# Two attention and feed-forward layers on one core: the first products of batch 14 over three heads, and the last layer's tokens in parts of 12 and 4 batches

## The chip, the cores and the metric

The kernel runs on one NeuronCore of one Trainium2 chip. The metric is the device time of one execution in microseconds (us); the time of the kernel before is 1855.08 us, the median of three runs (1853.94 to 1855.9). Batches and heads are counted from 0, so there are batches 0 to 15, and batch 14 is the next to last.

## The reference

The input `x` is 16 batches of 256 tokens with 256 features, and `ctx_1024` is a context of the same shape. Four layers follow one another, each added to `x`, each on the layer norm of `x`:

```python
x = x + xattn0(ctx_1024, layernorm(x), ...)   # 8 heads of 128, keys from the context and from x
x = x + ffn0(layernorm(x), ...)               # hidden 1024, weights W1 and W2 changed per batch by 16 of its tokens
x = x + xattn1(layernorm(x), ctx_1024, ...)   # one head of 256
x = x + experts(layernorm(x), ...)            # 8 experts with inner size 256
```

In the last layer each token has a weight for each of the 8 experts, which comes from its own router logits `z`:

```python
inh = sigmoid(x @ Wr / temperature)
in_zone = (inh >= GOLDEN_LOWER) & (inh <= 0.5)
w = exp(-abs(inh - GOLDEN_CENTER) / 0.1) * in_zone
# a token with no expert in the zone takes its best two instead
out = sum_e weights[e] * (silu(x @ Wg[e]) * (x @ Wu[e])) @ Wd[e]
```

A token is served by an expert where that weight is above zero. How many tokens an expert serves is decided by the data alone; it is not fixed at two or at any other number.

## The kernel before, in words

The whole program is written out as straight-line code by one Python function. Its order on each engine is the order in which the Python code issues instructions, because the schedule is manual. There is one `if` on the chip, at the very end.

**Heads.** The outer loop runs over `n`, the 16 x 8 heads of the first layer, with a pipeline in three stages: `s1` makes scores, `s2` writes their transposes to DRAM and `s2_fetch` reads them back, `s3` multiplies with the values. While batch b is in its heads, the later layers of batch b-1 run as a *chain* (`chain`, a generator) and the routing of a batch as a second generator (`route`). Both stand in a list `line`; `gap()` is called between the pieces of a head and takes units from the first job in `line` that is ready. What "ready" means is planned: every `yield w` in a generator tells that it can go on when the planned TensorE time `Clock.pe` has grown by `w`. The planned time grows by every matmul that is issued, in units that are not those of the chip. So a larger `yield` puts other instructions ahead of the next unit, and nothing else; the true waits are semaphores.

**The chain's feed-forward part.** Eight products `ph` (`W1e` with the tokens) come in four pairs, each followed by `yield 1.0`. Behind the last pair ScalarE takes a Gelu over all of `hT` (line 475). The second products `pf` need `hT` and `W2e`; `W2e` is made by GpSimd (by VectorE for batch 15) at line 437 and added up by VectorE at line 445. Ahead of `pf` stands `yield done[0] - Clock.pe`, which is the planned end of the Gelu.

**Routing.** `route` finds for each token which experts serve it, counts with a matmul by a triangle of ones how many came before it, and so gives every served (token, expert) a slot. GpSimd then writes the token's row (256 features, 8 weights, its number) with an indirect DMA into `slots_d` (line 719), once for each expert. Tokens that an expert does not serve go to slots counted from the end. `slots_d` has two parts, by batch, given by `PARTS`. Each part has for each expert as many slots as tokens, of which the first half, `CAPS`, is worked through in any case:

```python
PARTS = (10, 6)
NTOKS = [n * S for n in PARTS]
CAPS = [n // 2 for n in NTOKS]
```

For parts of 10 and 6 batches the capacities are 1280 and 768 tokens, that is 10 and 6 tiles of 128 rows for each expert, 128 tiles for all.

**The last layer.** `experts` is a generator over a list of *groups*. A group is 1 to 4 tiles of one expert and part. Its rows are loaded (line 1138, SyncE's queue), transposed in blocks by VectorE, written to DRAM (line 296) and read back (line 302) as `yTd`; then come the products `pg` and `pu`, tanh on ScalarE (line 1201), two operations on VectorE (lines 1211 and 1212) and, one group later, the products `pd`, one for each tile, whose weighted result `o` (line 1227) is added to the output in DRAM by an indirect DMA from GpSimd (line 1228). The chain before has written `x` to the output; every scatter adds to it. Scatters of one part and expert never meet in a row, nor do those of different parts; a scatter waits for the scatters of another expert of its own part. The rows of part 1 are loaded only once batch 15 has been routed (`ready` in `experts`).

The list before is: part 0 in groups of 4, 3 and 3 tiles for each expert, except the last group of expert 7; then part 1 in groups of 3 and 3 for experts 0 to 6; then the last group of part 0; then part 1 of expert 7 in 3, 2 and 1.

**The `if`.** After all this VectorE takes the slot counters, subtracts the limits, and takes the maximum over both parts and all experts (lines 1364 to 1366). Every engine loads that number (line 1367) and compares it (line 1368). Where any expert has more tokens in a part than the capacity, the block runs, and works through the other half of all slots, of every expert and both parts, with the same `experts` generator:

```python
some = nc.values_load(beyond[0:1, 0:1], min_val=0, max_val=1)
with tc.If(some > 0):
    drain(experts(groups(0, "+", (4, 3, 3)) + groups(1, "+", (3, 3))))
```

Of the kernel before, what the change touches and what calls it, by code (L numbers as in the profile page):

```python
# [29 lines left out]
def xattn_ffn_kernel(  # L30
# [11 lines left out]
    B, S, D = x.shape  # L42
# [4 lines left out]
    E = Wg.shape[0]  # L47
# [20 lines left out]
    def mm_tile(n, name):  # L68
        return psum.tile([P, n], F32, tag="mm", bufs=6, name=name, padded_shape=[P, 512])
# [9 lines left out]
    def mm(out, lhsT, rhs, **kw):  # L79
        nc.tensor.matmul(out, lhsT, rhs, **kw)  # L80
        Clock.pe += max(0.38, 1.667e-3 * math.prod(out.shape[1:]))
# [76 lines left out]
    )  # L158


    PARTS = (10, 6)
    NTOKS = [n * S for n in PARTS]
    CAPS = [n // 2 for n in NTOKS]

# [51 lines left out]
    def col(key, i):  # L216
        k, r = at[key]
        return cvecs[k][:, r + i : r + i + 1]
# [97 lines left out]
    def advance(gen):  # L316
        return gen is not None and next(gen, DONE) is not DONE

    def drain(gen):
        while advance(gen):  # L320
            pass
# [10 lines left out]
    def chain(b, A, behind):  # L332
# [60 lines left out]
        def rows_everywhere(half):  # L393
            evs.append(wk.tile([P, NI, D], F32, tag="ev", name=f"ev_{half}_{b}"))
            nc.sync.dma_start(
                evs[half].rearrange("p n d -> p (n d)"),
                ev_d[ts(half, NI)].rearrange("n d -> (n d)").partition_broadcast(P),
            )
            landed.append(Clock.pe + 8.0)
# [27 lines left out]
        def w1_rows(i):  # L427
            for d in range(DC):
                nc.vector.scalar_tensor_tensor(
                    W1e[:, d, i, :], evs[0][:, i, :], od[:, d, i : i + 1], W1T[:, d, ts(i, D)],  # L430
                    ALU.mult, ALU.add,
                )
# [21 lines left out]
        for k in range(HC):  # L454
            ph = mm_tile(S, f"ph_{b}_{k}")
            for d in range(DC):
                mm(
                    ph, W1e[:, d].rearrange("p i a -> p (i a)")[:, ts(k, P)], yT[:, d],
                    start=(d == 0), stop=(d == DC - 1),
                )  # L460
            nc.vector.tensor_scalar(hT[:, k, :], ph, col("b1", k), None, ALU.add)
            if k % 2 == 1:
                i = k // 2
                if i + 2 < NI:
                    w1_rows(i + 2)
                yield 1.0
                if i == 1:
                    rows_everywhere(1)
        A.fed.add(b)

        done = []
# [14 lines left out]
            w2_add(c)  # L486
        while not done:
            yield 0.2
        yield done[0] - Clock.pe
        W2r = W2e.rearrange("p c d o -> p (c d) o")  # L490
        mv = mv_tile("q")
        for c in range(TC):
# [136 lines left out]
    def route(b, A, mine):  # L629
        while not mine.done or (b >= 1 and not A.tails[b - 1].done):  # L630
            yield 0.4
        part = 0 if b < PARTS[0] else 1
        row = A.row[b]
# [105 lines left out]
    with ExitStack() as sh, ExitStack() as sa, ExitStack() as sf:  # L739
# [352 lines left out]
        def add_chain(b, behind):  # L1092
            job = Job(chain(b, A, behind))
            A.tails[b] = Job(route(b, A, job))
            line.extend([job, A.tails[b]])
            return job
# [20 lines left out]
        def load_expert(e):  # L1117
            k = len(D_.w)
            pool = D_.front if k == 0 else D_.wk if k == 1 else D_.more
            w = D_.w[e] = pool.tile([P, 3, DC, D], F32, bufs=1, name=f"wx_{e}")  # L1120
            nc.sync.dma_start(w[:, 0], Wg[e].rearrange("(c p) i -> p c i", p=P))
            nc.sync.dma_start(w[:, 1], Wu[e].rearrange("(c p) i -> p c i", p=P))
            nc.sync.dma_start(w[:, 2], Wd[e].rearrange("(c p) d -> p c d", p=P))
# [113 lines left out]
        def experts(groups, ready=None):  # L1237

            if groups[0].e not in D_.w:
                load_expert(groups[0].e)  # L1240
            for g in groups[:2]:
                g.load()
            yield 7.0
            while D_.wk is None:
                yield 0.4
            for d in range(DC):
                groups[0].turn_rows(d)
                yield 4.0
            late = None
            for n, g in enumerate(groups):  # L1250
                if n == 0:
                    groups[2].load()
                if n + 3 < len(groups):
                    while ready is not None and not ready(groups[n + 3]):
                        yield 0.4
                for i in range(IC):
                    g.gate(i)
                    yield
                    g.up(i)
                    yield  # L1260
                    if n == 0:
                        groups[1].turn_rows(i)
                    if n + 2 < len(groups):
                        if i == 0:
                            groups[n + 2].send_rows()
                        else:
                            groups[n + 2].fetch_rows()
                    if i == 0 and n + 3 < len(groups):
                        groups[n + 3].load()
                    if late is not None:  # L1270
                        late.down(2 * i)
                        late.down(2 * i + 1)
                        yield
                ahead = groups[min(n + 3, len(groups) - 1)].e
                if ahead not in D_.w and (len(D_.w) < 2 or D_.more is not None):
                    load_expert(ahead)
                if n + 2 < len(groups) and groups[n + 2].e not in D_.w:
                    while D_.more is None:
                        yield 0.4
                    load_expert(groups[n + 2].e)  # L1280
                late = g
            for t in range(late.tiles):
                late.down(t)

        def groups(part, more, sizes, experts_=range(E)):

            gs = []
            for e in experts_:
                t = CAPS[part] // P if more else 0
                for k in sizes:  # L1290
                    gs.append(G(part, e, t, k, more))
                    t += k
                assert t == NTOKS[part] // P if more else t == CAPS[part] // P
            return gs

        first = groups(0, "", (4, 3, 3))
        lists = (
            first[:-1] + groups(1, "", (3, 3), range(E - 1))  # L1300
            + first[-1:] + groups(1, "", (3, 2, 1), [E - 1])
        )

        last = None
        for n in range(NS + 2):
            b, h = divmod(n, H)
# [59 lines left out]
        nc.vector.tensor_scalar(beyond, most, 0.0, None, ALU.is_gt)  # L1366
        some = nc.values_load(beyond[0:1, 0:1], min_val=0, max_val=1)
        with tc.If(some > 0):
            drain(experts(groups(0, "+", (4, 3, 3)) + groups(1, "+", (3, 3))))


# [36 lines left out]
```

## Time and profile before

| quantity | value |
|---|---|
| median of three runs | 1855.08 us |
| the profiled execution's own time | 1854.39 us |
| its span in the trace | 1852.7 us |
| TensorE (PE) busy | 1810.5 us, 98% |
| VectorE (DVE) busy | 1208.8 us, 65% |
| GpSimd (POOL) busy | 852.1 us, 46% |
| ScalarE (ACT) busy | 582.6 us, 31% |
| moved by DMA | 332.72 MB, 180 GB/s over the span |
| scatters to `out_dram` (line 1228) | 128, 201.5 us on POOL |

An execution's time is a little longer than the span from its first to its last instruction (here 1.7 us). In lines of the trace, `PE L80 MATMUL` is a matmul at line 80, `out<-in` names the tiles, `x8` says that eight instructions are merged, the first two numbers are the start in us from the span's start and the duration, and a bracket at the end gives the idle time of the engine ahead of the line and what ended it. `SPq`, `POOLq` and the like are the sequencers of the engines, which issue instructions and DMAs. Each fp32 matmul in the program is two matmuls in the trace.

### The profile page before, as it was taken

The page shows a single profiled execution, that of the slowest core. Times are in us where ns is not written, and L with a number is a line of the kernel's source. Part 1 is how long each engine was busy: PE and PEld are TensorE (multiplying, and loading weights), DVE is VectorE, ACT ScalarE, POOL GpSimd, SP SyncE. Part 2 cuts the span into 40 slices and gives each one's busy share as a digit, 9 for nine tenths or more (in the row PEclk, how much of TensorE's full clock was granted, in tenths as well). Part 3 has the DMA queues.
Part 4 walks back from the last instruction along what each step waited for, and adds up shares of the span by engine and source line. Part 5 has one row for each costly group of instructions (what it writes and reads, how often), then busy time and mean ns, then how long its engine had stood idle before and what let it go on. Part 6 is the DMA issues. An engine that isn't in the chain of part 4 may idle for free. (4 is left out here: it accounts for less than half of the span.)

```text
span 1852.7 us, 22641 instructions
## 1 busy us (share of the span) xinstructions
PE 1810.5 (98%) x6600; PEld 1234.7 (67%) x6600; DVE 1208.8 (65%) x3341; ACT 582.6 (31%) x1298; POOL 852.1 (46%) x988
## 2 busy tenths in 40 slices
PE   8999999999999999999999999999998999999995
PEld 4666666666666666676767676767675766666664
DVE  5456585858585867676757676767666575665663
ACT  3443334343433333333333333333433211111110
POOL 2123235353535353535353535353525177766666
PEclk9999999999999999999999999999999999999997
DMA  6553546464646564546464646464636398999995
GB/s 222 181 180 125 159 154 206 150 198 154 197 160 198 160 195 163 193 160 198 154 205 143 207 145 206 146 212 143 205 110 223 95 234 190 244 248 221 211 204 83
DMA packets 271181, 332.72 MB, mean 180 GB/s; under 512 B 31388, under 2 KB 222792, under 8 KB 271048
## 3 DMA queue, kind: packets, MB, share of 16 engines
q1 hardware_dynamic: 240280, 279.63, 47.9%
q0 software_dynamic: 30720, 51.54, 12.0%
q8 instruction: 55, 0.90, 0.2%
q14 instruction: 78, 0.64, 0.1%
q10 hardware_dynamic: 48, 0.01, 0.0%
HBM read 165.77 MB, written 165.28 MB: 179 GB/s over the span
## 5 line engine op out<-in xcount | busy, mean ns | idle before, releaser
L903 POOL TENSOR_SCALAR pr<-pr,ri 128x512 f32<-128x512 f32 x256 | 179.5, 711 | 317.6 <-DVE ri L902 313.1
L895 ACT ACTIVATE pr<-sc,nm 128x512 f32<-128x512 f32 x256 | 173.5, 682 | 479.3 <-DVE nm L889 479.0
L719 POOL DMA_INDIRECT slots_d<-row,at_slot x256 | 253.2, 989 | 70.7 <-issue 69.8
L1228 POOL DMA_INDIRECT out_dram<-o,at x128 | 201.5, 1574 | 96.6 <-DVE o L1227 36.2
L80 PE MATMUL po<-pT,v 128*128 128x256 f32 x1024 | 243.2, 381 | 1.4 <-DMA pT<-hop 0.7
L80 PE MATMUL sc<-kT,qT 128*128 128x512 f32 x512 | 241.2, 594 | 1.5 <-ACT kT L828 1.5
L80 PEld LDWEIGHTS po<-pT,v 128*128 128x128 f32 x1024 | 195.4, 191 | 69.2 <-issue 36.0
L80 PE MATMUL pk<-kvT,Wk_sb 128*128 128x512 f32 x512 | 240.7, 593 | 0.0
L80 PE MATMUL pv<-Wv_sb,kvT 128*128 128x512 f32 x512 | 235.2, 593 | 0.0
L941 DVE TENSOR_SCALAR outT<-po,cvec 128x256 f32<-128x256 f32 x128 | 61.1, 477 | 258.3 <-PE po L80 258.2
L911 DVE STREAM_TRANSPOSE tb<-pr 128x512 f32<-128x512 f32 x256 | 165.9, 686 | 8.3 <-DMA hop<-tb 8.0
L80 PEld LDWEIGHTS pv<-Wv_sb,kvT 128*128 128x128 f32 x512 | 97.2, 190 | 107.2 <-issue 102.0
L889 DVE TENSOR_REDUCE nm<-sc 128x1 f32<-128x512 f32 x256 | 160.3, 663 | 2.0 <-PE sc L80 1.9
L80 PEld LDWEIGHTS sc<-kT,qT 128*128 128x128 f32 x512 | 97.0, 190 | 70.0 <-issue 61.2
L80 PEld LDWEIGHTS pk<-kvT,Wk_sb 128*128 128x128 f32 x512 | 97.5, 190 | 67.7 <-issue 61.1
L1201 ACT ACTIVATE sg<-pg 128x384 f32<-128x384 f32 (+3 forms) x82 | 41.3, 503 | 305.2 <-PE pg L80 305.2
L80 PE MATMUL pf<-W2e,hT 128*128 128x256 f32 x512 | 123.6, 391 | 10.4 <-ACT hT L475 7.1
L80 PE MATMUL pq<-kvT,Wq_sb 128*128 128x256 f32 x512 | 133.0, 382 | 0.0
L80 PE MATMUL pg<-yTd,wx 128*128 128x384 f32 (+3 forms) x328 | 123.9, 500 | 0.9 <-ACT yTd L826 0.9
L80 PEld LDWEIGHTS pq<-kvT,Wq_sb 128*128 128x128 f32 x512 | 96.6, 191 | 42.0 <-issue 28.4
L80 PE MATMUL pd<-wx,hTd 128*128 128x256 f32 x512 | 124.0, 380 | 0.2 <-DVE hTd L1212 0.2
L80 PE MATMUL pu<-yTd,wx 128*128 128x384 f32 (+3 forms) x328 | 123.6, 500 | 0.0
(205 smaller groups left out, 2655.8 us busy)
## 6 DMA issues: line engine op xcount, KB each, us to landing
hop<-tb SPq DMA_DIRECT2D x128, 512.0 KB
pT<-hop SPq DMA_DIRECT2D x512, 128.0 KB
ev<-ev_d SPq DMA_DIRECT2D x32, 512.0 KB
rows<-slots_d SPq DMA_DIRECT2D x31, 397.5 KB
hop_rows_b<-rows_b SPq DMA_DIRECT2D x30, 384.0 KB
yTd<-hop_rows_b SPq DMA_DIRECT2D x120, 96.0 KB
rows<-slots_d SPq DMA_DIRECT2D x8, 530.0 KB
cin<-in_ctx_dram SPq DMA_DIRECT2D x16, 256.0 KB
```

The costliest lines, as they stand in the source:

```text
L80: nc.tensor.matmul(out, lhsT, rhs, **kw)
L719: ins = nc.gpsimd.indirect_dma_start(out=slots_d[part], out_offset=bass.IndirectOffsetOnAxis(ap=at_slot[:, c, e : e + 1], axis=0), in_=row ...
L889: nc.vector.tensor_reduce(nm, sc, AX.X, ALU.max, negate=True)
L895: nc.scalar.activation(pr, sc, AF.Exp, bias=nm, accum_out=sm)
L903: nc.gpsimd.tensor_scalar(pr, pr, ri, 1.0, ALU.mult, ALU.mult)
L911: nc.vector.transpose(tb[:, :, c, :], heads[n][c][0].rearrange("p (m f) -> p m f", m=QP))
L941: nc.vector.tensor_scalar(o, po, col("bv", h), None, ALU.add)
L1201: nc.scalar.activation(self.sg, self.pg, AF.Tanh, scale=0.5)
L1228: ins = nc.gpsimd.indirect_dma_start(out=out_rows[0 : sum(NTOKS[: self.part + 1]), :], out_offset=bass.IndirectOffsetOnAxis(ap=self.at[:, ...
```

## The change

Four things are changed.

1. `PARTS` is (12, 4) in place of (10, 6). The capacities follow: 1536 and 512 tokens, 12 and 4 tiles for each expert, again 128 tiles in all.
2. In the chain of batch 14, each of the four pairs of `ph` is followed by `yield 4.5` in place of `yield 1.0`.
3. In the chain of batch 15, the wait ahead of `pf` is at least 5.0 planned units.
4. The list of groups: part 0 has three groups of 4 for experts 0 to 5, four groups of 3 for expert 6, and 3, 3, 2, 2, 2 for expert 7; part 1 is one group of 4 for each expert. The last eight groups of part 0 (three of expert 6 and five of expert 7) stand in turn with the eight of part 1: one of part 1, one of part 0, and so on. The list in the `if` block follows with groups of 4.

```diff
-    PARTS = (10, 6)
+    PARTS = (12, 4)
...
-                yield 1.0
+
+                yield 1.0 if b != B - 2 else 4.5
...
-        yield done[0] - Clock.pe
+        yield max(done[0] - Clock.pe, 5.0 if b == B - 1 else 0.0)
...
-        first = groups(0, "", (4, 3, 3))
-        lists = (
-            first[:-1] + groups(1, "", (3, 3), range(E - 1))
-            + first[-1:] + groups(1, "", (3, 2, 1), [E - 1])
-        )
+        first = groups(0, "", (4, 4, 4), range(E - 2))
+        first += groups(0, "", (3, 3, 3, 3), [E - 2]) + groups(0, "", (3, 3, 2, 2, 2), [E - 1])
+        second = groups(1, "", (4,))
+        lists, first = first[:-E], first[-E:]
+        for pair in zip(second, first):
+            lists += pair
...
-            drain(experts(groups(0, "+", (4, 3, 3)) + groups(1, "+", (3, 3))))
+            drain(experts(groups(0, "+", (4, 4, 4)) + groups(1, "+", (4,))))
```

## The prediction

> **What bounds the kernel now.** I read the page first, then the windows of the end, the TensorE and GpSimd timelines there, and the instructions of the `if`.
>
> ```profile
> PE   8999999999999999999999999999998999999995
> ...
> 1653.00:1753.00 100.00, 100.00 (x352) 66.70 (x351) 58.16 (x148) 12.68 (x25) 65.10 (x44) 1.00 0.96 220
> ```
> TensorE is full all along (98%). In the last stage it is busy 100 of 100 us at full clock, DMA at a share of 0.96 and 220 GB/s.
>
> ```profile
> 1434.71 3.78 PE L80 MATMUL pf<-W2e,hT 128*128 128x256 f32 x8 [7.14 <-ACT hT L475]
> 1438.29 2.89 PE L80 MATMUL po<-pT,v 128*128 128x256 f32 x8
> ...
> 1527.36 1.13 PE L80 MATMUL pf<-W2e,hT 128*128 128x256 f32 x4 [1.91 <-DVE W2e L445]
> 1529.81 7.56 PE L80 MATMUL pf<-W2e,hT 128*128 128x256 f32 x20 [1.32 <-DVE W2e L445]
> ```
> These are the holes that edits 2 and 3 aim at: the `pf` of batch 14 waits 7.14 us for the Gelu, that of batch 15 waits 3.2 us for `W2e`.
>
> ```profile
> 1652.20 1.88 PE L80 MATMUL pg<-yTd,wx 128*128 128x512 f32 x4
> 1653.92 1.88 PE L80 MATMUL pu<-yTd,wx 128*128 128x512 f32 x4
> 1655.63 1.89 PE L80 MATMUL pd<-wx,hTd 128*128 128x256 f32 x8
> ...
> 1661.66 1.46 PE L80 MATMUL pg<-yTd,wx 128*128 128x384 f32 x4
> 1662.95 1.46 PE L80 MATMUL pu<-yTd,wx 128*128 128x384 f32 x4
> 1664.24 1.89 PE L80 MATMUL pd<-wx,hTd 128*128 128x256 f32 x8
> ```
> Start to start: `pg` or `pu` of half a group takes 1.72 us with four tiles and 1.29 with three; `pd` of two tiles takes 1.72.
>
> ```profile
> 1764.79 1.56 POOL L1228 DMA_INDIRECT out_dram<-o,at  x1 [0.30 <-issue]
> 1770.87 1.56 POOL L1228 DMA_INDIRECT out_dram<-o,at  x1 [4.52 <-DVE o L1227]
> ...
> 1841.92 1.56 POOL L1228 DMA_INDIRECT out_dram<-o,at  x1 [0.30 <-issue]
> ```
> A scatter takes 1.56 + 0.30 = 1.86 us of GpSimd. At a change of expert there is a hole (4.52 here, 3.6 to 5.6 in part 1, on average 4.3 beyond the usual 0.30). The trace puts it down to VectorE, but it recurs just at these places, with `o` long made: I read it as the wait until the old expert's scatters have landed. So GpSimd runs behind: TensorE ends at 1831.1, the last scatter at 1843.5, the span 9.2 later.
>
> ```profile
> L1367 SPq TENSOR_LOAD <-beyond x1: 475/475/475, 1832.2 to 1832.2; - x1
> L1368 SPq COMPARE_BRANCH  x1: 50/50/50, 1833.0 to 1833.0; - x1
> L1368 PEldq COMPARE_BRANCH  x1: 4580/4580/4580, 1832.8 to 1832.8; - x1
> L1368 SPq EVENT_SEMAPHORE  x8: 17/17/17, 1836.3 to 1836.9; - x8
> ```
> The `if` is decided at 1832 to 1833. The block is skipped: no row of it follows.
>
> **Part 1: the capacity.** The block runs when one expert has more tokens in one part than half the part's tokens. The reference on its own inputs tells how many it has (weights above zero). In batches 10 to 15 the largest is expert 0 with 760 (capacity 768), in batches 0 to 9 it is 1099 (1280): the block is skipped, as the trace shows. In batches 0 to 11 the largest is 1340 (1536). In batches 12 to 15 the eight experts have 516, 325, 413, 400, 426, 452, 380 and 396. The capacity is 512. Expert 0 is 4 over; so `some` is 1, and the block works through the upper half of all slots: 24 groups of 4 tiles of part 0 and 8 of part 1, again 128 tiles. Would the chip count the same? For 512, four of the 516 have to fall out. Of expert 0's logits in these batches three lie within 0.001 of a limit of the zone, none within 0.0001. I take it that the block runs.
>
> **Part 2: the block's price.** A group of four is 4 x 1.72 + 2 x 1.72 = 10.32 us of TensorE, 2.58 a tile; of three, 4 x 1.29 + 3 x 0.86 = 7.74, 2.58 a tile too. So the new widths win TensorE nothing in the list (0), and 32 groups cost 330.2.
> - Entry. `beyond` is ready 1.0 after TensorE's end (1831.1 to 1832.1). Load, register operation and comparison take 0.8 on SyncE. Built, the block stands right behind the branch; not to jump is one comparison (0.05). Bounds: 0, and the 4.6 that TensorE's jump over the block took; I take 0. The Trainium skill ("Runtime: NRT & Kernel Launch", Instruction fetch mechanics) says that a taken branch out of the fetched pages stalls for a fetch; before, that was 3.2 to 4.6 us, at no cost behind GpSimd; by the rule the change would swap it to the block's end, worth nothing either way.
> - Rows. The first load (530 KB) has to land. A write of 384 KB in this stage let its reader go 2.7 to 3.4 us later; the nearest slow case is a rows load whose transposes begin 6.5 us after it. I take 4 (2.7 to 6.5). Transposes and ScalarE's copies until the first `pg`: 2.
> - Clock. TensorE idles about 8 us here. After the 7.14 us hole the same products ran at a granted 0.50: `pf` x8 took 3.58 for 1.72, `po` 2.72 for 1.72, so 2.9 lost. I take 2.9 (0 to 3.1, the loss at 1530). The Trainium skill ("TensorE: Matmul & The Clock Gate", What's actually happening) gives half clock for one window of about 3.4 us; that would lose 1.7, and the sum be 1.2 lower.
> - Transposes of the second group: 0.9.
> - Scatters. Part 0 gives GpSimd 12 x 1.86 + 4.3 = 26.6 us an expert against TensorE's 31.0: hidden. Part 1 changes expert with every group: 4 x 1.86 + 4.3 = 11.7 against 10.3, so GpSimd falls behind. From the last group's start to TensorE's end are 13.8 us of products, 4.8 of them (with VectorE's 0.5) ahead of the first `o` of the group before; so that `o` is ready 9.0 before the end, and the first of part 1 another 6 x 10.32 sooner, 70.9 before. 7 x 11.7 later GpSimd begins the last group, and 7.2 later ends it: 18.2 behind TensorE (5 if no hole came, 26 with holes of 5.6). The nearest row is the mean hole of part 1 before, so 18.2 stands. `o` has 18 buffers, so this doesn't stop TensorE. Then the same 9.2.
>
> **Part 3: the list's own part.** Edit 2 moves score products and one `po` ahead of the last `ph`, and puts `pg` and `pu` of the first group behind it: 10.8 us of work before `pf` in the built order, where there were 12.5. The maxima and exponentials ahead of the Gelu come earlier, but two copies of `ydT` (their DMA lands some 19 us after `po` of the second attention) and the first tanh now stand ahead of it, and `pl` waits for that copy: about 2.6 us stay of 7.14 + 2.9. Worth 7 (0 to 10). Edit 3 puts 15.8 us of products between `ph` and `pf` where 12.0 were; the hole there is 3.2 + 3.1 at half clock. Worth 5 (0 to 6.3). Together 12 (0 to 16.3).
> Edit 1 lets the first load wait for batches 10 and 11 too, a batch's time (some 96 us) after they are routed: 0. Part 1's first load (SyncE's queue) comes at tile 64 in place of 67, 7.7 us sooner. GpSimd ended its slot writes at 1670, 26 us ahead of that load: covered; uncovered it would hold SyncE's queue, and every later group's rows, by what is missing (0 to 10, in the range).
> The order in turn puts 3 or 2 scatters of the other part (5.6 or 3.7 us) into holes of about 4.3, so the backlog of 12.3 us goes. What is late next is TensorE. Without the block that would be worth 7 (the last four scatters still end 5 behind TensorE); with the block, which hides the backlog, nothing.
>
> **Sum.** 1831.1 - 12 + (1.0 + 0.8 + 4 + 2) + (330.2 + 2.9 + 0.9) + 18.2 + 9.2 = 2188.3 span; + 1.7 for what lies around it in the profiled execution (1854.39 against 1852.7), + 0.7 to the median: **2191 us**.
>
> **Rivals.**
> - *The block is not entered* (fewer than 513 tokens counted, or other inputs). For: the margin is 4. Against: none lies within 0.0001 of a limit. Then the list's own part is all there is: 1831.1 - 12 + 5 + 9.2 + 2.4 = 1836, 1% faster. The point is 512 counted tokens of expert 0; at 513 the whole price of the block is paid. It decides the sign alone.
> - *DMA bounds the block.* A group moves 530 + 3 x 512 KB; in 10.32 us that is 205 GB/s. For: the share is already 0.96. Against: 220 GB/s beside a full TensorE. At only the span's mean of 180 GB/s a group takes 11.75, 46 us more: 2237.
> - *The list wins nothing* (both holes stay): 2203, inside the range.
>
> **How the numbers follow.** Block entered and TensorE-bound 0.82 (2191; 2165 to 2228), DMA-bound or starved above that 0.10, not entered 0.08 (of which 0.01 no measurable change). The range adds the bounds: below, 4.3 of the holes, 2.9 of the clock, 1.3 of landing, 13.2 of the scatters and some 4 for products in the block that run unlike the rows: 26; above, 12 of the holes, 4.6 of entry, 2.5 of landing, 8 of scatters and 10 of SyncE's queue: 37. 0.2% is about what this kernel's measurement can tell. Faster 0.07, same 0.01, slower 0.92.
>
> **What would show it.** `pd` 1024 times in place of 512, scatters to `out_dram` 256 in place of 128, some 400 MB moved, rows of line 1228's successor until about 2179, TensorE ending near 2161, with one hole of 8 us from about 1819, and the hole of 7.14 us ahead of `pf` under 3. Wrong: no rows behind the branch; or groups in the block more than 10.4 us apart.

## The result, and the profile after

The changed kernel takes 2174.98 us (median of four runs, 2174.47 to 2176.34), the kernel before on the same chip 1855.28 us. The ratio is 1.1725, with a 95% interval of 1.1705 to 1.1746: the change makes the kernel 320 us slower. The span of the profiled execution is 2172.9 us. A kernel's time is the median of its runs; one run of the kernel with edits 2 and 3 alone, 2745.61 us at a granted clock of 0.65 (0.988 or more in all others), is left out of it. The order of the readings below is that of the prediction.

First the page of the changed kernel: the slices of TensorE, the totals of DMA, the scatters (busy us and mean ns ahead of the idle time before them) and the products `pd`.

```profile
PE   8999999999999999999999999999999998999996
...
DMA packets 323700, 398.18 MB, mean 183 GB/s; under 512 B 35260, under 2 KB 272104, under 8 KB 323560
...
L1229 POOL DMA_INDIRECT out_dram<-o,at x256 | 399.6, 1561 | 237.3 <-DVE o L1228 167.9
...
L80 PE MATMUL pd<-wx,hTd 128*128 128x256 f32 x1024 | 241.9, 379 | 0.0
```

The scatters are 256 where there were 128, `pd` 1024 where there were 512, and 398 MB are moved in place of 333. TensorE is as full as before (98%), but the span holds 320 us more of it: one tenth less in slice 34 (1793 to 1847 us) is the only mark in TensorE's row that something else begins there. That something is seen in the instructions of the `if`, at the lines of the load and of the comparison:

```profile
L1369 SPq TENSOR_LOAD <-beyond x1: 472/472/472, 1814.5 to 1814.5; - x1
...
L1370 PEldq COMPARE_BRANCH  x2: 87/134/180, 1815.2 to 2151.9; - x2
L1370 SPq COMPARE_BRANCH  x2: 38/44/49, 1815.4 to 2131.9; - x2
```

Each sequencer has two comparisons, one at 1815 and one where its part of the block ends (2132 to 2160). Before, there was one, and on TensorE's sequencer it took 4580 ns, the jump over the block. Now no comparison takes over 180 ns: the block is entered. TensorE's timeline shows what follows, and how the holes of edits 2 and 3 look:

```profile
1433.11 1.14 PE L80 MATMUL pl<-Wr_sb,ydT 128*128 128x8 f32 x8 [0.91 <-ACT ydT L827]
...
1438.01 1.89 PE L80 MATMUL pf<-W2e,hT 128*128 128x256 f32 x8
...
1519.59 7.07 PE L80 MATMUL pf<-W2e,hT 128*128 128x256 f32 x32
...
1809.89 3.62 PE L80 MATMUL pd<-wx,hTd 128*128 128x256 f32 x16
1820.95 1.97 PE L84 MATMUL rowsT<-ident,rows 128*128 128x128 f32 x8 [7.44 <-DMA rows<-slots_d]
1822.73 3.73 PE L80 MATMUL pg<-yTd,wx 128*128 128x512 f32 x4
1826.30 1.88 PE L80 MATMUL pu<-yTd,wx 128*128 128x512 f32 x4
...
2150.60 5.34 PE L80 MATMUL pd<-wx,hTd 128*128 128x256 f32 x24
```

Neither `pf` waits any longer (7.14 and 3.2 us before); 0.91 us is left, at `pl`. The list ends at 1813.5, TensorE idles 7.44 us until the block's rows have landed, and the block's products run from 1822.7 to 2155.9, that is 333.2 us. GpSimd's timeline at the end:

```profile
2138.12 1.55 POOL L1229 DMA_INDIRECT out_dram<-o,at  x1 [2.92 <-DVE o L1228]
...
2148.56 1.55 POOL L1229 DMA_INDIRECT out_dram<-o,at  x1 [3.04 <-DVE o L1228]
...
2159.00 1.55 POOL L1229 DMA_INDIRECT out_dram<-o,at  x1 [2.97 <-DMA out_dram<-o,at]
...
2164.57 1.55 POOL L1229 DMA_INDIRECT out_dram<-o,at  x1 [0.30 <-issue]
```

In the block's last quarter, part 1, experts change every four scatters, and the first scatters of an expert start 10.1 to 10.7 us apart, 10.37 on average: that is close to TensorE's pace (10.32 a group). The last scatter ends at 2166.1, 10.2 behind TensorE; the span ends 6.8 later.

### The profile page after: what moved, and what is told of

It is laid out like the page before. It is cut to its first block, busy times and chain, and to the rows that moved or that the text cites. A ratio compares the mean times of both kernels' runs of the same rounds, so it can differ in the third digit from the quotient of the medians.

```text
span 2172.9 us, 25665 instructions
## 1 busy us (share of the span) xinstructions
PE 2138.9 (98%) x7546; PEld 1409.6 (65%) x7546; DVE 1394.0 (64%) x3743; ACT 622.0 (29%) x1355; POOL 1050.3 (48%) x1116
## 4 chain that ended last, share of the span: by engine, by line
PE 96%; DMA 1%; DVE 1%; issue 0%; SPq 0%; POOL 0%; ACT 0%; POOLq 0%; ACTq 0%; DVEq 0%
PE po L80 11%; PE pv L80 11%; PE sc L80 11%; PE pg L80 10%; PE pu L80 10%; PE pd L80 10%; PE pk L80 10%; PE pq L80 6%; PE px L80 5%; PE pf L80 5%; PE ph L80 5%; PE pl L80 1%; DVE tb L912 0%; POOL out_dram L1229 0%; PE pn L80 0%
## 5 line engine op out<-in xcount | busy, mean ns | idle before, releaser
L1229 POOL DMA_INDIRECT out_dram<-o,at x256 | 399.6, 1561 | 237.3 <-DVE o L1228 167.9
L80 PE MATMUL pg<-yTd,wx 128*128 128x512 f32 (+2 forms) x536 | 243.8, 577 | 0.0
L80 PE MATMUL pd<-wx,hTd 128*128 128x256 f32 x1024 | 241.9, 379 | 0.0
L80 PEld LDWEIGHTS pd<-wx,hTd 128*128 128x128 f32 x1024 | 194.3, 190 | 73.2 <-issue 48.5
L80 PE MATMUL pu<-yTd,wx 128*128 128x512 f32 (+2 forms) x536 | 241.8, 573 | 0.0
L1202 ACT ACTIVATE sg<-pg 128x512 f32<-128x512 f32 (+2 forms) x134 | 77.4, 578 | 563.8 <-PE pg L80 513.1
L1212 DVE SCALAR_TENSOR_TENSOR sg<-sg,pg 128x512 f32<-128x512 f32 (+2 forms) x134 | 88.9, 663 | 185.5 <-ACT sg L1202 171.6
L80 PEld LDWEIGHTS pu<-yTd,wx 128*128 128x128 f32 x536 | 101.8, 190 | 116.2 <-issue 98.9
L912 DVE STREAM_TRANSPOSE tb<-pr 128x512 f32<-128x512 f32 x256 | 165.9, 686 | 12.3 <-DMA hop<-tb 8.5
L80 PEld LDWEIGHTS pg<-yTd,wx 128*128 128x128 f32 x536 | 101.5, 191 | 67.4 <-issue 55.5
```

Of the source, the lines that this page charges most:

```text
L912: nc.vector.transpose(tb[:, :, c, :], heads[n][c][0].rearrange("p (m f) -> p m f", m=QP))
L1202: nc.scalar.activation(self.sg, self.pg, AF.Tanh, scale=0.5)
L1212: nc.vector.scalar_tensor_tensor(sg, sg, 1.0, self.pg, ALU.add, ALU.mult)
L1229: ins = nc.gpsimd.indirect_dma_start(out=out_rows[0 : sum(NTOKS[: self.part + 1]), :], out_offset=bass.IndirectOffsetOnAxis(ap=self.at[:, ...
```

## The experiments

Theory: the whole loss is the `if` block, entered because expert 0 has 516 tokens in part 1 and room for 512; the rest of the change wins about 1%. Rivals: something else in the change (the list, the DMA) costs time too; or the chip enters the block for another reason.

**The block shut, and the number that opens it.** Two kernels differ from the changed one in one number each, how far over the limit an expert may be. The block then decides between them.

```diff
-        nc.vector.tensor_scalar(beyond, most, 0.0, None, ALU.is_gt)
+        nc.vector.tensor_scalar(beyond, most, 4.0, None, ALU.is_gt)
```

> The changed kernel with one number changed: the block is entered only where an expert is more than 4 tokens over its capacity (4.0 in place of 0.0), so up to 4 tokens of expert 0 lose that expert's share. Theory (the block is the whole loss, because expert 0 counts 516 on the chip too): the block is skipped, TensorE ends near 1813.5 as in the changed kernel's list, the last scatter near 1819, 9.2 more, about 1830 us. As the prediction's rival put it: 1836. Rival (the new list itself costs the time, or the count on the chip is above 516): 2175.

> The same with 3.0 in place of 0.0: no share is lost if the block runs. Theory: 516 is the count on the chip, 4 is more than 3, the block runs, about 2175 us. Rival (the chip counts 515 or fewer, the block ran by another margin than the reference's): skipped, about 1830 us.

With 4.0 the time is 1832.88 us (ratio to before 0.9881, interval 0.9865 to 0.9898); with 3.0 it is 2172.02 (one run). With 4.0 TensorE's sequencer jumps over the block again:

```profile
L1370 PEldq COMPARE_BRANCH  x1: 3962/3962/3962, 1818.7 to 1818.7; - x1
```

So the largest excess on the chip is exactly 4, which is that of the reference's 516 tokens of expert 0. The block costs 2174.98 - 1832.88 = 342.1 us, and everything else in the change together wins about 22 (the kernel before took 1854.80 beside the shut block).

**The price by group.** In this kernel the block works through part 1's eight groups alone, without the 24 of part 0.

```diff
-            drain(experts(groups(0, "+", (4, 4, 4)) + groups(1, "+", (4,))))
+            drain(experts(groups(1, "+", (4,))))
```

> The changed kernel with only part 1 in the block, the part that is over (8 groups of 4 in place of 32). Theory (the block costs TensorE 10.32 us a group, everything else in it is a fixed entry and end): 24 x 10.32 = 247.7 us less, about 1927 us. Rival (the block is bound by scatters or DMA or has a large fixed cost): its 32 groups do not cost in proportion, 1940 us or more.

Measured: 1928.88 us (1.0403, 1.0386 to 1.0421). The 24 groups left out cost 246.1 us, 10.25 each, against the 10.32 of TensorE that the prediction took. The eight that stay cost 96.0 over the shut block, 8 x 10.32 + 13.4: the 13.4 are what the block costs once (by the same sum it is 11.9 with all 32 groups).

**The hole at a change of expert.** Here part 1's groups have two tiles, taken in turn over the experts, so that the expert changes 16 times and GpSimd, not TensorE, sets the pace.

```diff
-            drain(experts(groups(0, "+", (4, 4, 4)) + groups(1, "+", (4,))))
+            pairs = groups(1, "+", (2, 2))
+            drain(experts(pairs[0::2] + pairs[1::2]))
```

> Part 1 alone in the block, in 16 groups of 2 tiles, all first halves of the experts and then all second halves, so that the expert changes every 2 scatters and GpSimd's wait at a change is laid bare. TensorE gives a group every 5.16 us; GpSimd needs 2 x 1.86 plus the wait beyond the usual 0.30. Theory (the wait is the landing of the last scatter, about 3.0 us after it where the DMA share is 0.8): 6.4 us a group, the last scatter 23 us behind TensorE, 13 us above the kernel with part 1 in groups of 4, about 1940 us. Rival (the prediction's 4.3 beyond the usual 0.30): 8.0 us a group, 47 us behind, about 1964 us.

Measured: 1952.71 us (one run), between the two expectations. GpSimd's timeline shows why there is no single number:

```profile
1894.52 1.55 POOL L1229 DMA_INDIRECT out_dram<-o,at  x1 [4.94 <-DVE hTd L1213]
1896.38 1.55 POOL L1229 DMA_INDIRECT out_dram<-o,at  x1 [0.31 <-DVE sg L1212]
...
1934.04 1.55 POOL L1229 DMA_INDIRECT out_dram<-o,at  x1 [2.95 <-DMA out_dram<-o,at]
1935.90 1.55 POOL L1229 DMA_INDIRECT out_dram<-o,at  x1 [0.30 <-issue]
1940.45 1.55 POOL L1229 DMA_INDIRECT out_dram<-o,at  x1 [3.00 <-DMA out_dram<-o,at]
```

The changes come 7.57 us apart from 1834 to 1894.5 and 6.56 apart from there to 1940.5. Taking off two scatters and the usual gap (2 x 1.55 + 0.31), the hole is 4.2 us at first and 3.2 later. In the windows of the same run the share of DMA falls from 0.80 (1850 to 1870) over 0.61 (1890 to 1910) to 0.35 (1920 to 1945), and the holes at the end, with nothing else to move, are 2.95 to 3.00. There the trace names the transfer itself. So the wait for the old expert's scatters to land is real, and about 3 us at least (2.88 is the shortest here); how much more it is varies.

**Edits 2 and 3 alone**, on the kernel before, with its parts and its list:

```diff
-                yield 1.0
+                yield 1.0 if b != B - 2 else 4.5
...
-        yield done[0] - Clock.pe
+        yield max(done[0] - Clock.pe, 5.0 if b == B - 1 else 0.0)
```

> The kernel before with edits 2 and 3 alone (parts of 10 and 6, the old list). Theory: both holes of TensorE go, it ends 15 us sooner, but GpSimd was full from 1545 on and its last scatter, 12.3 us behind TensorE before, hardly moves: 1850 to 1855 us. Rival (TensorE's end sets the end): 1840 us.

Measured: 1837.90 us (0.9918, 0.9903 to 0.9933). TensorE ends at 1818.0, which is 13.1 sooner than before. What I had expected of GpSimd's backlog was wrong, and the rival right: the last scatter ends only 6.2 us behind TensorE without any turn. Of the six that are gone from 12.3, three are gone behind the last slot write: the last eight holes have a mean of 4.36 where they had 4.61 (2.0 in all), and a scatter takes 1.54 in place of 1.56 (about 1 over the last 64). GpSimd thus needs 15.2 us for an expert of part 1 (6 x 1.85, and 4.06 that the hole is beyond the usual gap), where it needed the same 15.5 as TensorE, and catches up a little. The other three were won ahead of it: the last slot write starts 16.0 us sooner than before (at 1653.98, where it was 1669.98), which is 2.9 more than TensorE's end moved; why it moved by more is not shown.

**The list alone.** The changed kernel without edits 2 and 3, and with the block shut by 4.0 as above.

> The changed kernel with edits 2 and 3 undone (both yields as before) and the block kept shut by the threshold of 4.0, which leaves out the four slots of expert 0 that are over; so what is left of the change is the list alone: 12 and 4 batches, in turn. Theory (the list wins only by letting the scatters end close behind TensorE): the two holes before the first products come back, so TensorE ends where it did before, at about 1831, and with the 15.8 us from TensorE's end to the span's end that the changed kernel with the shut block had, the span is about 1847 and the time 1847 to 1850, ratio 0.997. Rival (any turn brings part 1's slot rows too soon, as with parts of 10 and 6 batches, where TensorE stood 15 us for them): 1862 or more. Second rival (the list of 12 and 4 wins TensorE time by itself): 1835 or less.

Measured: 1846.72 us (0.995, 0.9937 to 0.9964), as the theory said. TensorE's timeline has its old hole back, and ends at 1830.1 (1831.1 before); the last scatter ends 5.5 behind it.

```profile
1436.37 3.78 PE L80 MATMUL pf<-W2e,hT 128*128 128x256 f32 x8 [7.14 <-ACT hT L475]
...
1532.04 6.27 PE L80 MATMUL pf<-W2e,hT 128*128 128x256 f32 x20 [2.21 <-DVE W2e L445]
```

So groups of four win TensorE next to nothing (1.0 us); the list wins by what stands behind TensorE, where the backlog of 12.3 us has become 5.5.

**The turn with the old parts.** Would the gain of the turn be had without the 12 and 4? The list of 10 and 6 batches, with the last six groups of part 0 between part 1's experts, once without and once with edits 2 and 3:

```diff
-        first = groups(0, "", (4, 3, 3))
-        lists = (
-            first[:-1] + groups(1, "", (3, 3), range(E - 1))
-            + first[-1:] + groups(1, "", (3, 2, 1), [E - 1])
-        )
+        first = groups(0, "", (4, 3, 3), range(E - 1)) + groups(0, "", (2, 2, 2, 2, 2), [E - 1])
+        second = groups(1, "", (3, 3), range(E - 1)) + groups(1, "", (3, 2, 1), [E - 1])
+        lists, first = first[:-6], first[-6:]
+        for k in range(E):
+            lists += second[2 * k : 2 * k + 2] if k < E - 1 else second[2 * k :]
+            lists += first[k : k + 1]
```

> The kernel before with its old parts of 10 and 6 and only the list changed: expert 7 of part 0 in five groups of 2, and six groups of part 0 set between the experts of part 1. TensorE's work is the same. Theory (the backlog of GpSimd at changes of expert sets the end): last scatter about 5 behind TensorE's 1831, 1848 us. Rival (the end is not set by those waits): 1855 us.

> Edits 2 and 3 and the list in turn, with parts of 10 and 6, so the block stays skipped. Theory: TensorE 15 us sooner and the scatters at its heels, 1831 - 15 + 5 + 9.2 + 2.4, about 1833 us, more than the two edits alone bring together. Rival (what one edit wins the other loses, or the two just add): 1840 us or above.

Both theories failed, and of the rivals only that of the second run holds (1840 or above: the gain of edits 2 and 3 is lost again). Without edits 2 and 3 the time is 1866.05 us (1.0067, 1.0052 to 1.0081), slower than before; with them 1850.80 (0.9987, 0.9976 to 0.9998). The scatters do end 5.4 behind TensorE, but TensorE has a new hole (its timeline, run without the edits):

```profile
1676.11 2.90 PE L80 MATMUL pg<-yTd,wx 128*128 128x384 f32 x4 [15.06 <-DVE o L1227]
```

The engine that the trace names had nothing to do with it; SyncE's queue in the same run shows the cause:

```profile
1648.94 0.34 SPq L296 DMA_DIRECT2D hop_rows_b<-rows_b  x1
1670.10 0.38 SPq L1138 DMA_DIRECT2D rows<-slots_d  x1
1670.57 1.85 SPq L302 DMA_DIRECT2D yTd<-hop_rows_b  x4
```

The load of part 1's first rows usually follows the write of `hop_rows_b` by 0.05 us. Here it is held for 20.8 us, until GpSimd has written batch 15's slots (the last of those writes starts at 1667.44), and behind it in the queue stands the reading of `yTd` that the next products need. In this list the load is issued after 57 tiles; before, it was after 67, in the changed kernel after 64. One more kernel tests that: as the one with edits 2 and 3, but with four groups in the turn, and so the load after 64 tiles.

```diff
-        lists, first = first[:-6], first[-6:]
+        lists, first = first[:-4], first[-4:]
...
-            lists += first[k : k + 1]
+            lists += first[k - 3 : k - 2] if k >= 3 else []
```

> The kernel before with edits 2 and 3 and with parts of 10 and 6 batches in turn, as in the run that stood 15 us for part 1's rows, but with four of part 0's groups between part 1's experts (behind experts 3 to 6) in place of six, so that part 1's first load is issued after 64 tiles (as in the changed kernel) and not after 57. Theory (the stall is only part 1's slot rows written too late for that load): the hole of 15 us goes, TensorE ends near 1818 as with the edits 2 and 3 alone, the last scatter 5 to 6 behind, time about 1836 to 1838, ratio 0.990. Rival (the turn itself, two experts of two parts at once, is what holds TensorE): 1848 or more.

Measured: 1840.25 us (0.9921, 0.9905 to 0.9938). The hole of 15 us is gone, so the load's place was its cause. The load is still held, for 6.5 us in place of about 21. The time is two to four above what I expected: TensorE now ends near 1825, with five small waits for `yTd` (4.8 us in all, the longest 2.1). The turn with the old parts thus wins nothing over edits 2 and 3 alone (1837.90).

**Two ways to have room.** The whole change, but with room for 11 and 5 tiles for each expert (1408 and 640 tokens) and groups of 4, 4, 3 and 3, 2 (expert 7 of part 0 in 3, 2, 2, 2, 2), the last six of part 0 in turn with part 1's experts. The block stays shut, 128 tiles as before, and its list follows.

```diff
-    CAPS = [n // 2 for n in NTOKS]
+    CAPS = [11 * P, 5 * P]
```

> The whole change, but with room for 1408 and 640 tokens per expert instead of 1536 and 512 (11 and 5 tiles, 128 tiles in all as before), which holds the largest counts of 1340 and 516, so that the block stays shut with nothing left out. Groups (4,4,3) and (3,2) in turn, part 1's first load at tile 63. Theory: the same work as with the shut block, so 1833, at most 8 us more for the eight further expert groups' weights of small size and for a part 1 that is a quarter larger. Rival (part 1's expert changes, five scatters each, now hold up the scatters): 1845 or more.

Measured: 1845.82 us (0.9952, 0.9937 to 0.9967). The rival had the number, but not the reason: the scatters end 5 us behind TensorE, while TensorE ends near 1829, 12 later than with the shut block. From 1400 to 1800 it is idle for 9.3 us, against 1.6 there; 3.7 of that are one wait for `yTd` and 3.7 two waits for VectorE ahead of transposes. Where the other four of the 12 went is not shown.

The other is the kernel before with its parts of 10 and 6, edits 2 and 3, and only as many tiles as the largest counts (1099 and 760) need: 9 and 6, which makes 120 tiles. The list is part 0, then part 1.

```diff
-    CAPS = [n // 2 for n in NTOKS]
+    CAPS = [9 * P, 6 * P]
...
-        first = groups(0, "", (4, 3, 3))
-        lists = (
-            first[:-1] + groups(1, "", (3, 3), range(E - 1))
-            + first[-1:] + groups(1, "", (3, 2, 1), [E - 1])
-        )
+        first = groups(0, "", (3, 3, 3))
+        lists = first + groups(1, "", (3, 3), range(E - 1)) + groups(1, "", (3, 2, 1), [E - 1])
```

(The list of the block follows with groups of 4, 4, 3 and 3, 3, and the yield between a batch's slot writes is 2.6 for all batches, where it was 5.2 for the last two.)

> Edits 2 and 3, parts of 10 and 6, capacities of 9 and 6 tiles (1152 and 768 tokens; the largest counts are 1099 and 760) in place of 10 and 6, so 120 tiles in place of 128; the list is part 0 and then part 1; the slot writes of the last two batches are planned twice as close. Theory: 8 x 2.58 = 20.6 us less of TensorE than with 128 tiles, about 1812 to 1820 us, with GpSimd a little behind. Rival (part 1's rows come too late, since 8 tiles less of part 0 stand ahead of them): TensorE waits up to 20 us, 1835 us.

Measured: 1827.47 us (0.9863, 0.9847 to 0.9879), the fastest of all and faster than both kernels. It is not the full 20.6 us of eight tiles better than edits 2 and 3 alone, but 10.4: TensorE is idle for 10.9 us between 1340 and 1740 here, and for 3.3 there, 7.7 of the 10.2 that are missing.

## Why the prediction was right

The mechanism was right: the capacity of 512, the count of 516, the entry, and the price. The shut block shows that it is the whole loss, and the two limits show the count. The steps, in the order of the sum:

- *The list's end* was to be 1819.1 and is 1813.5. The term of 12 us for the two holes measured 13 to 18: 13.1 with edits 2 and 3 alone, 14.1 with the shut block, 17.6 here. The last two run the same instructions up to the comparison, so some 3.5 of the 17.6 are not the edits' doing. For `pf` of batch 14 the prediction left 2.6 us of the hole and of the half clock; 0.91 us is left.
- *Entry* at nothing was right (0.04 to 0.09 us for each engine's comparison, and at most 0.18 at the block's end). With the shut block TensorE's sequencer again takes 3.96 us for the jump. Of the Trainium skill's stall after a taken branch ("Runtime: NRT & Kernel Launch", Instruction fetch mechanics) the jump may be an instance; in the block that runs, no such stall shows, neither at its entry nor at its end.
- *Rows*: the block's first load is issued at 1815.48, and TensorE's transposes begin at 1820.95, 5.5 us later, where 4 was taken (2.7 to 6.5).
- *The clock*: the transposes and `pg` ran at a granted 0.50 from 1820.95 to 1826.30 and took 1.78 + 3.57 for 0.88 + 1.72, so 2.75 us lost. The row of the earlier hole gave 2.9, the estimate from the Trainium skill's window of about 3.4 us ("TensorE: Matmul & The Clock Gate", What's actually happening) 1.7: the row was nearer.
- *The block's products*: 334.0 predicted, 333.2 measured. Groups of four at 2.58 us a tile held for all 32, beside a DMA share of 0.82 to 0.89; so the rival that DMA bounds it fell.
- *Scatters behind TensorE*: 18.2 predicted, 10.2 measured. This is the mis-sized term. The step took the mean hole of the old list's part 1 (4.6 us, with the usual gap) for the block, so that GpSimd would need 11.7 us for a group against TensorE's 10.3 and fall behind by 1.4 at each. The seven holes between the experts of the block's part 1 are 2.92 to 3.48 us, 3.08 on average: at 3.1 GpSimd needs 4 x 1.55 + 3 x 0.30 + 3.1 = 10.2 a group, and keeps up.
- *The end*: 9.2 us from the last scatter to the span's end were taken over, 6.8 are measured. GpSimd's sequencer shows where those 2.4 went. Before, the last scatter lands at about 1845.8, an `INC_SWDGE_SEM` of 1.30 us follows at the line of the `if`, and only then a drain of 4.65 (the shut block has the same, 1.29 and 4.57). Where the block runs there is no such instruction at the `if`, the drain has been waiting since 2160.3, and it ends 3.6 behind the landing (about 2168.5).

These make -5.6 + 1.4 - 0.8 - 8.0 - 2.4 = -15.4 between the predicted span of 2188.3 and the measured 2172.9.

What the shorter holes are is seen in VectorE's timeline. The trace puts six of the seven down to `o`, but the `o` of the scatter at 2148.56, shown further up with its hole of 3.04, is made by 2146.99:

```profile
2146.51 0.48 DVE L1228 TENSOR_SCALAR o<-pd,wt 128x256 f32<-128x256 f32 x1 [0.18 <-PE pd L80]
```

Where GpSimd in this block starts as soon as it has `o`, it starts 0.28 us behind it; at these seven scatters it starts 0.6 to 5.1 behind. So these holes too are the wait for the old expert's scatters, as the prediction had read it, and only their size was wrong. Why they are 4.6 on average in the one place and 3.1 in the other no run isolates. The share of DMA within the holes themselves goes the same way in three runs: it is 0.38 to 0.61 in these seven (2.92 to 3.48 us), 0.71 to 0.93 in the six between part 1's experts in the old list (3.58 to 5.56 us), and in the kernel with pairs 0.73 to 0.95 at the holes of 3.2 to 4.9 and 0.41 at two of 2.9 to 3.0.

One step was wrong without cost. Part 1's first load was to be covered by 26 us of slack, since GpSimd had ended its slot writes at 1670. SyncE's queue in the changed kernel:

```profile
1650.01 0.34 SPq L296 DMA_DIRECT2D hop_rows_b<-rows_b  x1
1656.29 0.37 SPq L1139 DMA_DIRECT2D rows<-slots_d  x1
1656.79 2.27 SPq L302 DMA_DIRECT2D yTd<-hop_rows_b  x4
```

The load was held for 5.9 us. The slack of 26 was a misreading: counted through, part 1's first load in the kernel before is the one that SyncE issues at 1677.21, 7 us behind the start of the last slot write (1669.98); and since a load that is held goes 2.5 to 5.2 us behind that start in ten runs (1656.29 behind 1652.89 here), 2 to 5 were to spare. In the changed kernel the last slot write starts 17 us sooner (1652.89; 1653.98 with edits 2 and 3 alone, 1667.44 with the turn alone), but the load's turn comes some 27 sooner. TensorE had enough in hand and did not stop. Seven tiles earlier, in the list of 10 and 6 with six groups in turn, a wait of the same kind cost 15 us.

The prediction also took the 12.3 us of backlog as something that only the turn removes. Edits 2 and 3 remove half of it by themselves. Its sum for the shut block, 1836, is still only three above the measured 1832.88, since either way the scatters end close behind TensorE (5 in the sum, 5.6 measured); the largest difference is TensorE's end, 1817.1 where the sum has 1819.1.

## What to carry to other kernels

Where a kernel has a rare path guarded by a count, a change of a size that the guard is derived from has to be worked out on the data first: four tokens out of 516 decided 342 us here, no view of the kernel before has a row of it, and the same arithmetic showed room for eight tiles less, which made the fastest version. When a group is moved up in a list, count through to the first load that depends on a late writer: its place in an in-order queue, not its own length, decides what it stops.

## What was not expected of the hardware

- The same accumulating scatter's landing was waited for 2.88 to 5.6 us, with a floor near 3.0 that three runs share (2.94 to 3.06 at the very end of the changed kernel, of the block of eight groups and of the pairs). While it is waited for, the trace often names VectorE's `o`.
- A jump over the block took TensorE's sequencer 3.96 to 4.58 us in two kernels that skip it (before, and the shut block), and entering it 0.09. In both the jump ends no later than GpSimd's last scatter (1837.4 before 1843.5, and 1822.65 before 1822.66), so it costs nothing here; a kernel that ends with TensorE was not run.
- A load held in SyncE's queue for 20.8 us showed on TensorE as a wait for VectorE's `o`; only the queue's own rows told the cause.
